# Keys' ends for two tiles at once, a norm product on VectorE, a bf16 bias and routing weights in eight transfers

## The chip, the cores and the metric

The kernel runs on one core of a Trainium2 chip. The metric is device time in microseconds (us), as the median of several executions. Besides the times there is one profiled execution, whose instructions, waits and transfers can be read one by one. The engines are called PE (TensorE), DVE (VectorE), ACT (ScalarE), POOL (GpSimd) and SP (SyncE, which here issues nearly all transfers).

## The reference

The input is 16 images of 64 x 64 pixels and 128 channels, in float32. Two layers follow each other; only the second is touched by the change.

```
x = x + deform(groupnorm(x))          # 3x3 convolution gives offsets, x is sampled there
t = tokens(x)                         # 4096 tokens of 128 channels per image
t = t + attn(layernorm(t))
t = t + experts(layernorm(t))

attn:    q, k, v = split(n @ w_qkv + b_qkv)      # 8 heads of 16 channels, per token
         a[i, j] = softmax_j(scale * q[i] * k[j])   # 16 x 16 scores within one head of one token
         out = (a @ v) @ w_proj + b_proj
experts: p = softmax over the tokens of n @ gate_w.T + gate_b      # 64 experts
         each expert pools its 8 best tokens by p, runs a two-layer network on the sum,
         and its output is added to those tokens, weighted by p
```

## The kernel before

**Stages.** `Images` goes through the 16 images: the first and the last as code of their own, the 14 between as the body of a loop (line 1261). `finish` then runs the experts' networks and adds their outputs. Setup (weights, masks, constants) stands in `Images.__init__`.

**Chunks and slots.** An image has 4096 pixels in `NCH` = 8 chunks of 512. A chunk takes 32 steps of the sampling, done two at a time: PE spreads the row coordinates (`yps` from `parts` and `sel`, bf16), ACT makes ramps of them (`rhat`) and of the column coordinates (`chat`, loaded by SP from `cc_d`), PE multiplies (`yps` from `rhat` and `xr`), DVE multiplies both (`prod`), and PE sums (`acc`). The convolution of the next chunk (`cbank`), the attention of the chunks before (`tokens`), the norm of the next image (`prep`) and the routing of the image before (`tail`) run beside it.

**Tokens of a chunk.** The 512 tokens are four tiles of 128 (`a` = 0 to 3). `tokens` transposes, adds the residual, normalizes, and for each tile multiplies by `wqkv` on PE (`qkv_mm`, into `bank` for even tiles and `bank2` for odd ones) and adds the bias on DVE (`qkv_add`). The softmax needs the largest score for each query. So `end(a, 0)` takes the smallest key of each head on DVE (`kmm`), `shift` subtracts it from the keys on POOL, `end(a, 1)` takes the largest shifted key, `tops` multiplies it by the query on POOL, and ACT's Relu makes the largest score of it (`top`). Then, for each half of a tile, POOL makes the 16 x 16 scores of four heads (two instructions of 128 x 1024 on `sc`), ACT takes the exponential, DVE sums (`den`), POOL weighs with the values (`ev`), and DVE sums again (`att`). Before `proj` the result is transposed; `proj` sums bias and product for each tile in PSUM, 32 output rows at a time (`by_columns`). A second layer norm (`layer_norm` with `dst`) needs -mean/std for each token (`nmr`): `root` computes the inverse deviation on POOL by a power (`rstd`) and then `nmr` in two more POOL instructions, and ACT applies both (`xln`).

**Routing.** `tail` finds each expert's 8 best tokens in `logits`, marks them in `big` (also called `mark` there), and scales eight blocks of 512 columns on ACT (`scale`). When all are scaled, one transfer stores all 64 x 4096 weights to `wt_d`.

**Order.** Nothing of an image is emitted as it is written. Every operation is recorded with a slot (32 to a chunk, one for each step of the sampling), and `Work.order` plans the image: each engine takes, of what is ready by the planner's own durations, what starts first, with the slot as a handicap (`HASTE`). Operations put in by `plan.together` stay together. The queues of the engines then run strictly in the planned order, SP's too. A change of a slot, or of an operation's size, therefore moves instructions on every engine. In the profile all of them carry line 203, where they are emitted, so groups must be told apart by their tiles. PE runs each float32 matmul as two instructions with a weight load each; the counts of the profile are of those.

Of the kernel before, what the change touches and what calls it, by code (L numbers as in the profile page):

```python
# [10 lines left out]
BF16 = mybir.dt.bfloat16  # L11
I32 = mybir.dt.int32
AF = mybir.ActivationFunctionType
ALU = mybir.AluOpType
AX = mybir.AxisListType
# [4 lines left out]
P = 128  # L20
B, IMG, C = 16, 64, 128
NPIX = IMG * IMG
# [4 lines left out]
HEADS, HD = 8, 16  # L27
# [19 lines left out]
def bcast(ap, axis, n):  # L47

    shape = list(ap.shape)
    return ap.unsqueeze(axis).to_broadcast(shape[:axis] + [n] + shape[axis:])  # L50


def at_image(ap, b):

    return ap[b : b + 1] if isinstance(b, int) else ap[ds(b, 1)]


def by_columns(nc, out, weights, moving, start=True, stop=True):

    for c in range(0, out.shape[0], 32):  # L60
        nc.tensor.matmul(
            out[c : c + 32], weights[:, c : c + 32], moving, start=start, stop=stop)
# [315 lines left out]
class Images:  # L378
# [8 lines left out]
    def __init__(self, ctx, tc, x, conv_w, conv_b, w_qkv, b_qkv, w_proj, b_proj, gate_w, gate_b,  # L387
# [3 lines left out]
        nc = tc.nc  # L391
# [8 lines left out]
        ps = ctx.enter_context(tc.tile_pool(name="imgp", bufs=1, space=PSUM))  # L400
# [7 lines left out]
        def keep(shape, name, dtype=F32):  # L408
            return cp.tile(shape, dtype, name=name)
# [12 lines left out]
        for v in range(4):  # L422
            for m in range(4):
                at, c = slice(32 * v + m, 32 * (v + 1), 4), channel(0, v, m)
# [18 lines left out]
        nc.vector.tensor_scalar(self.bqkv[:, 0], self.bqkv[:, 0], C ** -0.5, None, ALU.mult)  # L443
        self.wproj = keep([P, C], "wproj")
        nc.sync.dma_start(self.wproj, w_proj)
        self.bproj = keep([P, C], "bproj")
        nc.sync.dma_start(self.bproj, b_proj.partition_broadcast(P))
        graw = keep([E, C], "graw")
        nc.sync.dma_start(graw, gate_w)
        self.gb = keep([E, 1], "gb")  # L450
# [50 lines left out]
        for g in range(4):  # L501
            for t in range(3):
                at = 32 * g + 8 * t
# [17 lines left out]
                         stop=True)  # L521
# [5 lines left out]
        for o in range(2):  # L527
# [5 lines left out]
            for g in range(4):  # L533
                for r in range(2):
                    at = 32 * g + 24 + r
# [31 lines left out]
        for m in range(4):  # L567
            nc.vector.memset(self.red[m], 0.0)
            for v in range(4):
                a, h = divmod((v - m) % 4, 2)  # L570
                at = 14 + 16 * a + h
# [366 lines left out]
    def layer_norm(self, src, dst, plan, slot):  # L938


        nc, mv, rstd = plan, self.mv, self.rstd[dst is not None]

        def stats(a):
            nc.vector.bn_stats(self.lst[:, a, :], src[:, a, :])
            nc.vector.bn_aggr(mv[:, a, :], self.lst[:, a, :])

        def root():
            nc.gpsimd.tensor_scalar(rstd, mv[:, :, 1], LN_EPS, None, ALU.add)
            nc.gpsimd.tensor_tensor(rstd, rstd, self.half, ALU.pow)
            if dst is not None:  # L950
                nc.gpsimd.tensor_scalar(self.nmr, mv[:, :, 0], -1.0, None, ALU.mult)
                nc.gpsimd.tensor_tensor(self.nmr, self.nmr, rstd, ALU.mult)

        def scale(a):
            nc.scalar.activation(
                dst[:, a, :], src[:, a, :], AF.Identity, bias=self.nmr[:, a : a + 1],
                scale=rstd[:, a : a + 1])

        for a in range(NA):
            plan.add(slot + a // 2, lambda a=a: stats(a))  # L960
            if dst is not None:
                plan.add(slot + 2, lambda a=a: scale(a))
        plan.add(slot + 1, root)
# [4 lines left out]
    def tokens(self, b, k, slot, dense=False, alone=HEADS):  # L968
# [14 lines left out]
        def add(rel, fn):  # L983
            plan.add(slot + rel, fn)
# [30 lines left out]
        def heads(s, a):  # L1015
            return self.qkv[:, a, s].rearrange("p (h d) -> p h d", d=HD)

        def tile_of(ap, a):
            return ap[:, HEADS * a : HEADS * (a + 1)]

        def qkv_mm(a):
            by_columns(nc, (self.bank, self.bank2)[a % 2][:, : 3 * C], t1T[:, a, :], self.wqkv)

        def qkv_add(a):
            nc.vector.scalar_tensor_tensor(
                self.qkv[:, a].rearrange("p s c -> p (s c)"),
                (self.bank, self.bank2)[a % 2][:, : 3 * C], self.rstd[0][:, a : a + 1],
                self.bqkv.rearrange("p s c -> p (s c)"), ALU.mult, ALU.add)

        def end(a, i):
            nc.vector.tensor_reduce(
                tile_of(self.kmm[:, i, :], a), heads(1, a), AX.X, ALU.max if i else ALU.min)

        def shift(a):
            nc.gpsimd.tensor_tensor(
                heads(1, a), heads(1, a), bcast(tile_of(self.kmm[:, 0, :], a), 2, HD),
                ALU.subtract)

        def tops(a):
            nc.gpsimd.tensor_tensor(
                tile_of(top, a), heads(0, a), bcast(tile_of(self.kmm[:, 1, :], a), 2, HD),
                ALU.mult)


        def group(i):
# [28 lines left out]

        for a in range(NA):
            at = 8 * a
            plan.together(slot + at + 7.5, lambda: qkv_mm(a))
            add(at + 8, lambda: qkv_add(a))  # L1080
            add(at + 9, lambda: end(a, 0))
            add(at + 9.5, lambda: shift(a))
            add(at + 10, lambda: end(a, 1))
            add(at + 10.5, lambda: tops(a))
            add(at + 11, lambda: nc.scalar.activation(tile_of(top, a), tile_of(top, a), AF.Relu))
            for i in (2 * a, 2 * a + 1):
                add(12 + 4 * i, lambda: score(i))
                add(14 + 4 * i, lambda: expo(i))
                add(16 + 4 * i, lambda: weigh(i))
            add(at + 20, lambda: nc.vector.reciprocal(tile_of(den, a), tile_of(den, a)))  # L1090
            add(at + 23, lambda: divide(a))
# [6 lines left out]
        def proj():  # L1098
            for a in range(NA):
                ps = self.bank[:, P * a : P * (a + 1)]  # L1100
                by_columns(nc, ps, self.ident, self.bproj, stop=False)
                by_columns(nc, ps, attT[:, a, :], self.wproj, start=False)

        def second():
# [29 lines left out]
    def tail(self, b, slot, turns):  # L1134
# [25 lines left out]
        def scale(k):  # L1160
            ks = slice(CHW * k, CHW * (k + 1))
            nc.scalar.activation(mark[:, ks], mark[:, ks], AF.Identity, scale=self.rsum)

        plan.add(slot, best)
        plan.add(slot + 4, lambda: nc.vector.match_replace(mark, self.top8, logits, HUGE))
        for k in range(NCH):
# [1 line left out]
            plan.add(slot + 8 + 2 * k, lambda k=k: choose(k))  # L1168
            plan.add(slot + 25 + k, lambda k=k: scale(k))
        plan.add(slot + 24, total)  # L1170
        plan.add(slot + 33, lambda: nc.sync.dma_start(
            at_image(self.wt_d, b).rearrange("b e n -> (b e) n"), mark))


        def load(i):
# [16 lines left out]
        def add(i):  # L1192
            for g in range(2 * NA):
                by_columns(
                    nc, self.bank2[:, :E], self.xl[:, g // NA, g % NA, :],
                    self.wt[:, E * g : E * (g + 1)],
                    start=(g == 0), stop=(g == 2 * NA - 1))

        def keep(i):
            if i == 0:  # L1200
                nc.vector.tensor_copy(self.pool_sum, self.bank2[:, :E])
            else:
                nc.vector.tensor_tensor(self.pool_sum, self.bank2[:, :E], self.pool_sum, ALU.add)
            if i == NCH // 2 - 1:
                nc.vector.tensor_copy(
                    self.pooled[:, :, b : b + 1] if isinstance(b, int)
                    else self.pooled[:, :, ds(b, 1)], self.pool_sum.unsqueeze(2))
# [269 lines left out]
```

## Time and profile before

| | us |
|---|---|
| median of 3 runs | 9108.26 |
| lowest, highest | 9106.29, 9114.67 |
| the profiled execution | 9137.11 |
| its span, first to last instruction | 9135.3 |
| mean granted TensorE clock in it | 0.951 of full speed |

In a group's row, `out<-in` names the tiles, the sizes are partitions x elements, and behind the count stand the busy time in us, the mean ns of one instruction, and the idle time of the engine just before them with what ended most of it. In the timeline the first two columns are start and duration in us; equal instructions that follow each other are merged, and brackets hold the idle time before them and what ended it. In a table of stages the columns are the stage, its length, busy us of PE, PE's weight loads, DVE, ACT and POOL with the number of instructions, the granted clock, the DMA engines' busy share and GB/s. SPq is SP's queue, where transfers are issued.

The images fill the span from about 80 to 8690 us; the experts' stage takes the rest.

### The profile page before, as it was taken

To read this page: it belongs to the slowest core of one execution; us is meant where nothing else is said; L and a number is where in the kernel's file an instruction comes from. 1 tells how busy PE (TensorE), PEld (TensorE's weight loads), DVE (VectorE), ACT (ScalarE), POOL (GpSimd) and SP (SyncE) were. 2 spreads that over 40 slices of the span, in tenths; PEclk is the share of its full clock that TensorE was granted. 3 is DMA by queue.
4 is the path that set the end of the run, shared out by engine and by line. 5 is a ranking of instruction groups with operands and counts; after the bars stand their busy time and mean duration, and the time that the engine had idled before them with its cause. 6 is when DMAs were issued, how large, how long until landed. Compare 5 with 4: busy or idle time off the path is not lost. (4 is left out here: it accounts for less than half of the span.)

```text
span 9135.3 us, 466677 instructions
## 1 busy us (share of the span) xinstructions
PE 8158.9 (89%) x205574; PEld 4234.3 (46%) x205574; DVE 7263.5 (80%) x10177; ACT 6534.8 (72%) x8082; POOL 7620.6 (83%) x5699
## 2 busy tenths in 40 slices
PE   6999999999999999999999999999899999989464
PEld 3544445454454545444454544445454544544234
DVE  3888888888888888888888888888888888888713
ACT  3877777777777778777777777777777777778400
POOL 1988888989898998989889898989989898989700
PEclk8999999999999999999999999999999999999756
DMA  5766766766676666766666766667676666666278
GB/s 140 190 176 181 189 174 187 186 183 184 177 192 176 187 185 186 186 177 186 181 186 183 191 182 180 187 176 192 178 197 179 182 188 176 190 174 182 80 234 294
DMA packets 1048563, 1678.95 MB, mean 184 GB/s; under 512 B 442480, under 2 KB 660336, under 8 KB 1041328
## 3 DMA queue, kind: packets, MB, share of 16 engines
q1 hardware_dynamic: 1024688, 1613.25, 64.7%
q8 instruction: 1616, 26.48, 1.3%
q10 hardware_dynamic: 21760, 35.14, 1.1%
q14 instruction: 499, 4.09, 0.2%
HBM read 1378.68 MB, written 268.96 MB: 180 GB/s over the span
## 5 line engine op out<-in xcount | busy, mean ns | idle before, releaser
L203 DVE SCALAR_TENSOR_TENSOR prod<-chat,yps 128x1024 f32<-128x1024 f32 x2048 | 2462.8, 1205 | 746.0 <-PE yps L203 214.2
L203 ACT ACTIVATE rhat<-yps 128x1024 f32<-128x1024 f32 x2048 | 2088.3, 1021 | 1296.4 <-PE yps L203 1197.7
L203 PEld LDWEIGHTS yps<-rhat,xr 32*32 32x32 f32 x131072 | 2172.1, 104 | 1525.7 <-ACT rhat L203 703.2
L203 PE MATMUL yps<-rhat,xr 32*32 32x176 f32 (+1 forms) x131072 | 2590.3, 275 | 277.6 <-ACT rhat L203 187.1
L203 PE MATMUL cbank<-pad,wconv 128*32 128x512 f32 x18432 | 2526.2, 621 | 34.6 <-DVE far L203 27.2
L203 POOL TENSOR_TENSOR ev<-sc,qkv 128x1024 f32<-128x1024 f32 x1019 | 2424.8, 2380 | 125.7 <-ACT sc L203 115.4
L203 POOL TENSOR_TENSOR sc<-qkv 128x1024 f32<-128x1024 f32 x1019 | 1977.7, 1941 | 57.6 <-POOLq L1261 19.1
L203 POOL TENSOR_TENSOR sc<-sc,top 128x1024 f32<-128x1024 f32 x1019 | 1988.2, 1953 | 17.8 <-ACT top L203 5.9
L203 DVE TENSOR_REDUCE att<-ev 128x64 f32<-128x1024 f32 x1024 | 1235.5, 1206 | 119.5 <-POOL ev L203 71.9
L203 ACT ACTIVATE chat<-chat,cbi,csc 128x1024 f32<-128x1024 f32 x1024 | 1261.4, 1237 | 56.0 <-DMA chat<-cc_d 50.9
L203 DVE TENSOR_REDUCE den<-sc 128x64 f32<-128x1024 f32 x1024 | 1237.9, 1209 | 63.9 <-ACT sc L203 61.2
L203 ACT ACTIVATE sc<-sc 128x1024 f32<-128x1024 f32 x1024 | 1076.0, 1051 | 220.6 <-POOL sc L203 144.2
L203 PE MATMUL acc<-prod,red 128*32 128x512 f32 x8192 | 1156.0, 617 | 39.6 <-DVE prod L203 37.7
L203 ACT ACTIVATE chat<-chat,cbi 128x1024 f32<-128x1024 f32 x1024 | 1161.2, 1143 | 33.2 <-DMA chat<-cc_d 31.8
L203 PE MATMUL yps<-parts,sel 32*32 32x512 bf16 x16384 | 932.6, 390 | 194.6 <-DVE prod L203 167.9
L203 PEld LDWEIGHTS cbank<-pad,wconv 128*32 128x32 f32 x18432 | 487.3, 110 | 839.0 <-issue 729.4
L203 PEld LDWEIGHTS <-sel 32*32 32x32 bf16 x16384 | 293.4, 88 | 991.1 <-issue 952.4
L203 DVE RECIPROCAL den<-den 128x128 f32<-128x128 f32 x512 | 480.4, 938 | 6.5
L203 DVE SCALAR_TENSOR_TENSOR qkv<-bank,rstd,bqkv 128x384 f32<-128x384 f32 x512 | 312.3, 610 | 194.4 <-PE bank L203 181.1
L203 PE MATMUL bank<-wqkv,tr 128*32 128x384 f32 x4096 | 440.6, 497 | 14.5 <-DVE qkv L203 11.6
L203 POOL TENSOR_TENSOR qkv<-qkv,kmm 128x128 f32<-128x128 f32 x512 | 219.7, 429 | 217.4 <-DVE kmm L203 214.8
L203 PEld LDWEIGHTS acc<-prod,red 128*32 128x32 f32 x8192 | 185.9, 109 | 347.9 <-issue 286.4
(166 smaller groups left out, 7699.8 us busy)
## 6 DMA issues: line engine op xcount, KB each, us to landing
chat<-cc_d SPq DMA_DIRECT2D x8192, 128.0 KB
xr<-xn_d SPq DMA_DIRECT2D x512, 128.0 KB
pc_d<-pc SPq DMA_DIRECT2D x512, 96.0 KB
parts<-pc_d SPq DMA_DIRECT2D x512, 96.0 KB
xl<-in_x_dram SPq DMA_DIRECT2D x128, 256.0 KB
xres<-in_x_dram SPq DMA_DIRECT2D x256, 128.0 KB
xn_d<-wt SPq DMA_DIRECT2D x128, 256.0 KB
cc_d<-cd SPq DMA_DIRECT2D x128, 256.0 KB
```

Source lines behind the costliest of these rows:

```text
L203: getattr(engine, fn)(*args, **kwargs)
```

## The change

There are four edits.

- **Bias.** The bias of the projection was a float32 tile, broadcast to 128 partitions, and was multiplied by the identity. Now setup splits it into three bf16 values whose sum is the float32 one to rounding, in rows 0 to 2 of a bf16 tile that is otherwise zero, and PE multiplies that by a 128 x 32 tile of bf16 ones.
- **Norm product.** `nmr` is one DVE instruction in place of two of POOL.
- **Two tiles at once.** `end`, `shift`, `tops` and the Relu each handle tiles 0 and 1, or 2 and 3, in one instruction. The slots of `qkv_mm` and `qkv_add` of an odd tile move to one behind those of the even tile, and the second pair's slots move 3.7 earlier.
- **Eight transfers.** Each of the eight blocks of the routing weights is stored on its own, recorded right behind its scaling, and the one store is gone.

```diff
@@ -443,8 +443,18 @@
         nc.vector.tensor_scalar(self.bqkv[:, 0], self.bqkv[:, 0], C ** -0.5, None, ALU.mult)
         self.wproj = keep([P, C], "wproj")
         nc.sync.dma_start(self.wproj, w_proj)
-        self.bproj = keep([P, C], "bproj")
-        nc.sync.dma_start(self.bproj, b_proj.partition_broadcast(P))
+        self.bproj = keep([P, C], "bproj", BF16)
+        self.ones3 = keep([P, 32], "ones3", BF16)
+        nc.vector.memset(self.bproj, 0.0)
+        nc.vector.memset(self.ones3, 1.0)
+        rest = self.big[0:1, 3 * NPIX // 4 + P :][:, :C]
+        part = self.big.bitcast(BF16)[0:1, 2 * (3 * NPIX // 4 + P + C) :][:, :C]
+        nc.sync.dma_start(rest, b_proj.unsqueeze(0))
+        for i in range(3):
+            nc.vector.tensor_copy(part, rest)
+            nc.sync.dma_start(self.bproj[i : i + 1], part)
+            if i < 2:
+                nc.vector.tensor_tensor(rest, rest, part, ALU.subtract)
         graw = keep([E, C], "graw")
         nc.sync.dma_start(graw, gate_w)
         self.gb = keep([E, 1], "gb")
@@ -948,8 +958,8 @@
             nc.gpsimd.tensor_scalar(rstd, mv[:, :, 1], LN_EPS, None, ALU.add)
             nc.gpsimd.tensor_tensor(rstd, rstd, self.half, ALU.pow)
             if dst is not None:
-                nc.gpsimd.tensor_scalar(self.nmr, mv[:, :, 0], -1.0, None, ALU.mult)
-                nc.gpsimd.tensor_tensor(self.nmr, self.nmr, rstd, ALU.mult)
+                nc.vector.scalar_tensor_tensor(
+                    self.nmr, mv[:, :, 0], -1.0, rstd, ALU.mult, ALU.mult)
 
         def scale(a):
             nc.scalar.activation(
@@ -1015,8 +1025,8 @@
         def heads(s, a):
             return self.qkv[:, a, s].rearrange("p (h d) -> p h d", d=HD)
 
-        def tile_of(ap, a):
-            return ap[:, HEADS * a : HEADS * (a + 1)]
+        def tile_of(ap, a, n=1):
+            return ap[:, HEADS * a : HEADS * (a + n)]
 
         def qkv_mm(a):
             by_columns(nc, (self.bank, self.bank2)[a % 2][:, : 3 * C], t1T[:, a, :], self.wqkv)
@@ -1029,19 +1039,27 @@
 
 
 
+        def ends(a, i):
+            return tile_of(self.kmm[:, i, :], a, 2).rearrange("p (a h) -> p a h", a=2)
+
+        def both(s, a):
+            return self.qkv[:, a : a + 2, s].rearrange("p a (h d) -> p a h d", d=HD)
+
         def end(a, i):
-            nc.vector.tensor_reduce(
-                tile_of(self.kmm[:, i, :], a), heads(1, a), AX.X, ALU.max if i else ALU.min)
+            nc.vector.tensor_reduce(ends(a, i), both(1, a), AX.X, ALU.max if i else ALU.min)
 
         def shift(a):
             nc.gpsimd.tensor_tensor(
-                heads(1, a), heads(1, a), bcast(tile_of(self.kmm[:, 0, :], a), 2, HD),
-                ALU.subtract)
+                both(1, a), both(1, a), bcast(ends(a, 0), 3, HD), ALU.subtract)
 
         def tops(a):
             nc.gpsimd.tensor_tensor(
-                tile_of(top, a), heads(0, a), bcast(tile_of(self.kmm[:, 1, :], a), 2, HD),
-                ALU.mult)
+                tile_of(top, a, 2).rearrange("p (a h) d -> p a h d", a=2), both(0, a),
+                bcast(ends(a, 1), 3, HD), ALU.mult)
+
+        def signs(a):
+            v = tile_of(top, a, 2)
+            nc.scalar.activation(v, v, AF.Relu)
 
 
         def group(i):
@@ -1076,13 +1094,15 @@
 
         for a in range(NA):
             at = 8 * a
-            plan.together(slot + at + 7.5, lambda: qkv_mm(a))
-            add(at + 8, lambda: qkv_add(a))
-            add(at + 9, lambda: end(a, 0))
-            add(at + 9.5, lambda: shift(a))
-            add(at + 10, lambda: end(a, 1))
-            add(at + 10.5, lambda: tops(a))
-            add(at + 11, lambda: nc.scalar.activation(tile_of(top, a), tile_of(top, a), AF.Relu))
+            early = at - 7 * (a % 2) - 3.7 * (a > 1)
+            plan.together(slot + early + 7.5, lambda: qkv_mm(a))
+            add(early + 8, lambda: qkv_add(a))
+            if a % 2 == 0:
+                add(early + 9.1, lambda: end(a, 0))
+                add(early + 9.5, lambda: shift(a))
+                add(early + 10, lambda: end(a, 1))
+                add(early + 10.5, lambda: tops(a))
+                add(early + 11, lambda: signs(a))
             for i in (2 * a, 2 * a + 1):
                 add(12 + 4 * i, lambda: score(i))
                 add(14 + 4 * i, lambda: expo(i))
@@ -1098,7 +1118,9 @@
         def proj():
             for a in range(NA):
                 ps = self.bank[:, P * a : P * (a + 1)]
-                by_columns(nc, ps, self.ident, self.bproj, stop=False)
+                for c in range(0, P, 32):
+                    nc.tensor.matmul(
+                        ps[c : c + 32], self.ones3, self.bproj, start=True, stop=False)
                 by_columns(nc, ps, attT[:, a, :], self.wproj, start=False)
 
         def second():
@@ -1160,6 +1182,8 @@
         def scale(k):
             ks = slice(CHW * k, CHW * (k + 1))
             nc.scalar.activation(mark[:, ks], mark[:, ks], AF.Identity, scale=self.rsum)
+            nc.sync.dma_start(
+                at_image(self.wt_d, b).rearrange("b e n -> (b e) n")[:, ks], mark[:, ks])
 
         plan.add(slot, best)
         plan.add(slot + 4, lambda: nc.vector.match_replace(mark, self.top8, logits, HUGE))
@@ -1168,8 +1192,6 @@
             plan.add(slot + 8 + 2 * k, lambda k=k: choose(k))
             plan.add(slot + 25 + k, lambda k=k: scale(k))
         plan.add(slot + 24, total)
-        plan.add(slot + 33, lambda: nc.sync.dma_start(
-            at_image(self.wt_d, b).rearrange("b e n -> (b e) n"), mark))
 
 
         def load(i):
```

## The prediction

> **What bounds the kernel now.** I read the page's busy times first, then one image by itself, then the waits, and last the two places where the change is heaviest. On the page TensorE leads, and GpSimd is close behind it:
>
> ```profile
> PE 8158.9 (89%) x205574; PEld 4234.3 (46%) x205574; DVE 7263.5 (80%) x10177; ACT 6534.8 (72%) x8082; POOL 7620.6 (83%) x5699
> ```
>
> These shares mix the images with the setup and the expert stage. The copies into the tile norm start one image after the other, 526.8 to 532.8 us apart. The table of stages over one of these periods gives:
>
> ```profile
> core 0: us, PE busy (x) PEld busy (x) DVE busy (x) ACT busy (x) POOL busy (x), PEclk, DMA share, GB/s
> 4341.10:4870.70 529.60, 492.84 (x12744) 252.72 (x12740) 444.34 (x619) 407.20 (x505) 477.13 (x356) 0.98 0.68 184
> ```
>
> Idle per image: PE 37 us, POOL 52, DVE 85, ACT 122. Both PE and POOL are nearly full, so work taken from one alone would soon meet the other. PE is tighter, and the waits agree: ACT's largest wait is for PE (rhat <- PE yps, 1197.7 us in all), while PE waits 168 us for DVE's prod. I take PE as the bound and POOL as the next.
>
> Next, a place that recurs. In the timeline, the store of the routing weights is one transfer of 1024 KB, and PE stops soon after it:
>
> ```profile
> 4011.79 0.58 SPq L203 DMA_DIRECT2D wt_d<-big  x1
> ...
> 4016.84 1.04 PE L203 MATMUL yps<-rhat,xr 32*32 32x176 f32 x41
> ...
> 4017.88 1.93 POOL L203 TENSOR_TENSOR sc<-sc,top 128x1024 f32<-128x1024 f32 x1
> ...
> 4021.27 0.48 PE L203 MATMUL yps<-rhat,xr 32*32 32x80 f32 x23 [3.38 <-issue]
> ...
> 4021.86 1.22 DVE L203 SCALAR_TENSOR_TENSOR prod<-chat,yps 128x1024 f32<-128x1024 f32 x1 [4.40 <-issue]
> ```
>
> "issue" says that no semaphore held PE: 41 of 64 matmuls of one step had run, the other 23 came 3.38 us later. The stages around it:
>
> ```profile
> 4010.00:4014.00 4.00, 4.00 (x117) 1.88 (x120) 3.16 (x4) 3.82 (x6) 4.00 (x3) 1.00 0.86 247
> 4014.00:4018.00 4.00, 3.89 (x133) 2.12 (x110) 2.42 (x3) 4.00 (x6) 4.00 (x4) 1.00 1.01 252
> 4018.00:4021.20 3.20, 0.00 (x0) 0.00 (x0) 0.00 (x0) 1.14 (x2) 3.20 (x3) 1.00 0.88 243
> ```
>
> The DMA engines are full (1.01) from 4014 to 4018, and between 4009 and 4018 the DMA view has no packet of the instruction queue, which over the span brings one every 5.7 us (1616 packets). In each of the 14 images of the loop PE stops about 9.5 us after this store, for 2.5 to 3.9 us (median 3.4). I read it as instructions that came late behind the store; the trace shows the order, not the cause.
>
> **The change, part by part.** *Bias as bf16 rows.* Now each 32-column quarter multiplies a float32 identity by the broadcast bias. The timeline of one projection:
>
> ```profile
> 4257.42 0.40 PE L203 MATMUL bank<-wproj,tr 128*32 128x128 f32 x8
> ...
> 4257.64 0.40 PE L203 MATMUL bank<-bproj,ident 128*32 128x128 f32 x8
> ...
> 4257.86 0.40 PE L203 MATMUL bank<-wproj,tr 128*32 128x128 f32 x8
> ```
>
> Starts are 0.22 us apart, so the four bias groups of a chunk take 0.87 us; there are 8 chunks in 16 images, 128 in all. The new group has four bf16 instructions instead of eight. Float32 matmuls of 512 and 128 columns last 617 and 273 ns, 0.90 ns a column over a fixed 156; bf16 ones of 512 columns last 390, so about 0.46 ns a column by the same fixed part. That makes 128 x 0.46 = 58 ns a group, and saves 4 x (215 - 58) = 0.63 us a chunk: 80 us. If bf16 brings nothing but half the instructions, 4 x 108 = 0.43 us: 55 us. A penalty for changing type between groups I leave out, because bf16 sel matmuls and float32 mains of the same 32*32 tiling already start within 20 ns of each other (4016.82 and 4016.84). All of it is on PE, which sets the pace: -80.
>
> *Eight transfers.* The stores become 128 KB each, one behind each of ACT's eight scalings, which the built order spreads over 46 SP transfers. No burst of 1 MB is left, so I take the stall as gone: 14 x 3.4 = -47; 0 if it only moves. SP gets 112 more issues of 0.58 us, 64 us in all. They are moved in among the column loads (chat<-cc_d), and each now waits for its ACT scaling with those loads behind it. What covers this is SP's own slack: it waits 1408 us for DVE's prod to free column buffers. I charge 0; were the cover gone, the eight waits of an image would cost ACT and DVE what they wait for these loads now once more, 83 and 95 us together at most, of which I keep 30 for the range.
>
> *Ends, shift and largest scores for two tiles; the norm product.* The rows:
>
> ```profile
> L203 DVE TENSOR_REDUCE kmm<-qkv 128x8 f32<-128x128 f32 x1024 | 284.7, 278 | 29.9 <-POOL qkv L203 15.7
> L203 POOL TENSOR_TENSOR qkv<-qkv,kmm 128x128 f32<-128x128 f32 x512 | 219.7, 429 | 217.4 <-DVE kmm L203 214.8
> L203 POOL TENSOR_TENSOR top<-qkv,kmm 128x128 f32<-128x128 f32 x512 | 209.9, 410 | 23.1 <-DVE kmm L203 21.3
> L203 POOL TENSOR_SCALAR nmr<-mv 128x4 f32<-128x4 f32 x128 | 31.1, 243 | 8.9
> L203 POOL TENSOR_TENSOR nmr<-nmr,rstd 128x4 f32<-128x4 f32 x128 | 25.9, 202 | 10.6
> ```
>
> GpSimd takes 1941 ns for 1024 elements (sc<-qkv) and 429 for 128, so 1.69 ns an element: 256 elements cost 645 (shift) and 626 (tops). Saved: 220 - 256 x 0.645 = 55, 210 - 256 x 0.626 = 50, and 57 of nmr; 162 us on POOL, 10.1 an image. DVE's ends: 679 ns for 512 elements (far) against 278 for 128 give 1.04 an element, 412 for 256; 512 of them are 211 us, 74 less. ACT's Relu: 512 x 303 become 256 x 410 (slope from 1051 ns at 1024), 50 less, beside other work.
>
> PE loses 5.0 us an image from the bias and 3.4 from the stall, 8.4 together; POOL loses 10.1. The smaller relief decides, so POOL's saving earns nothing of its own but keeps POOL from taking over. That is also its cover: were POOL unrelieved, its 52 us idle would have to absorb 8.4.
>
> The new waits: the shift waits for both tiles' ends, and behind it on POOL stand the scores of the other group. The matmuls and additions of the second tile of a pair come earlier in the built order, next to the first's; no instruction of theirs is added. I charge 0 here and price it as a rival.
>
> The norm product now stands on DVE between rstd's power on POOL and xln on ACT, and behind it in DVE's queue stands prod, for which PE waits. It reads two SBUF operands. How such small instructions last here:
>
> ```profile
> L203 DVE TENSOR_TENSOR gmv<-gmv x32: 158/622/1853, 95.4 to 7912.4; 128x1 f32<-128x1 f32 x32
> ...
> L203 DVE TENSOR_TENSOR farthest<-farthest,most x16: 758/1522/1535, 533.6 to 8469.5; 128x1 f32<-128x1 f32 x16
> ...
> L1274 DVE TENSOR_TENSOR worst<-worst,farthest x1: 146/146/146, 8471.3 to 8471.3; 128x1 f32<-128x1 f32 x1
> ```
>
> The columns are shortest/median/longest in ns. The last, with GpSimd idle, takes 146 ns; the first two, of the same shape, up to 1853 beside a busy GpSimd. I take the mean of the two medians, 1.07 us: 128 x 1.07 = 137 us, so DVE ends 63 us above today, 4 an image against 85 idle. What reaches PE lies between 0 and 137. PE had to wait for prod at 173 of 2048 steps, so most delays should be absorbed; I charge a quarter, +34.
>
> A rule of the Trainium skill speaks against this edit: "SBUF — State Buffer", section "Who interferes with whom", says that a VectorE instruction with two SBUF inputs contends with a GpSimd instruction that reads SBUF, and that whoever is first holds the shared ports for its whole instruction. These three rows agree with it. By the rule alone each product could wait out a full score (1.94 us): an estimate of 128 x 1.94 = 248 us of DVE time.
>
> *Setup.* The bias is split into three rows through a chain of copies and transfers. In the built order three more SP issues (0.55 us each) and the first eight sel stores (4.97 us) stand ahead of the first image load, now at 24.48 us; the second, at 30.66, moves little. Between 2 and 7 us, once: +5.
>
> Sum: -80 - 47 + 34 + 5 = -88. The profiled execution has a span of 9135.3 and took 9137.1 us, 28.9 above the median of the three runs, 9108.3. By it the sum gives 9049; I carry the difference over to the median: 9108 - 88 = 9020.
>
> **The rivals.** *POOL sets the pace.* Then its 10.1 us an image count, and the stall too, since after it POOL waits 4.7 us for mv: 13.5 x 15.5 = -209, 8899. For it: the 236 us that POOL waits for kmm should shrink with half the handshakes. Against: POOL idles more than PE.
>
> *The pair comes late.* The first score of a pair waits for the second tile too: 0.85 us of matmuls (wqkv), 0.61 of qkv addition, 0.13 of longer reduction, 1.6 us. POOL waited for kmm in 139 of 1024 cases; if a quarter of 256 pairs show the whole, +102, which eats the gain: 9122.
>
> *The product blocks DVE (slower).* Each product waits out a GpSimd instruction and PE waits for the prod behind it: 128 x 1.85 = 237 in place of the 34: 9108 - 122 + 237 = 9223. It decides from 122 / 128 = 0.95 us a chunk that reaches PE. For it: POOL is busy 90% of an image, and its next instruction starts as soon as the power is done. Against: DVE's 85 us of idle time.
>
> **How the numbers follow.** The forecast has 0.57, with its own range of 8960 to 9080 (bias 55 instead of 80, the stall half or wholly gone, the product 0 to 80). POOL sets the pace: 0.17. The late pair: 0.16, spread over 0.03 faster, 0.08 same, 0.05 slower. The blocked DVE: 0.10, slower. A measurement of this kernel tells about 0.2%, 18 us, from no change. Faster 0.57 + 0.17 + 0.03 = 0.77; same 0.08; slower 0.15. The range reaches from POOL's case, 8905, to just past the late pair, 9130.
>
> **What would show it.** Right: bias groups about 0.06 us apart from the wproj group behind them; no PE gap of 2 us or more marked issue behind a wt_d store; nmr on DVE near 1 us; POOL busy near 467 us an image; periods near 524. Wrong: periods unchanged with PE idle above 45 us, which would point at the pair (POOL qkv <- DVE kmm up) or at nmr (above 1.5 us, PE <- DVE prod up); or a stall of like size at another store or load.

## The result, and the profile after

The changed kernel takes 9148.87 us (median of 6 runs, 9134.15 to 9163.08), the kernel before 9109.19 (6 runs, 9106.29 to 9117.26). The ratio is 1.0043, 95% interval 1.003 to 1.0056: slower by 0.4%, where I forecast 1% faster.

The profiled execution of the changed kernel took 9146.53 us, 2 below its median; that of the kernel before, 9137.11, stands 28 above its own. So the two traces differ by 9 us only, and comparing them understates the loss. The kernel before took 9130 to 9141 us at the median on the five chips of the experiments below, so 9137 is an ordinary time for it there; on which chip its trace was taken the record doesn't say. The runs carry the verdict, and the traces are read for where time lies.

The page's busy times after:

```profile
PE 8113.1 (89%) x203526; PEld 4178.5 (46%) x203526; DVE 7306.4 (80%) x9800; ACT 6534.0 (71%) x7826; POOL 7481.9 (82%) x4931
```

PE has 46 us less to do and POOL 139 less, as the edits intended. Now the groups that the prediction priced (out<-in with sizes, count | busy, mean ns | idle before them):

```profile
L203 DVE TENSOR_REDUCE kmm<-qkv 128x16 f32<-128x256 f32 x512 | 212.4, 415 | 11.4 <-POOL qkv L203 3.1
...
L203 POOL TENSOR_TENSOR qkv<-qkv,kmm 128x256 f32<-128x256 f32 x256 | 165.4, 646 | 177.0 <-DVE kmm L203 176.8
L203 POOL TENSOR_TENSOR top<-qkv,kmm 128x256 f32<-128x256 f32 x256 | 160.1, 625 | 10.0 <-DVE kmm L203 9.8
...
L203 ACT ACTIVATE top<-top 128x256 f32<-128x256 f32 x256 | 106.2, 415 | 65.8 <-POOL top L203 65.3
```

415, 646, 625 and 415 ns, against 412, 645, 626 and 410 worked out beforehand. The projection in the timeline of PE:

```profile
4255.00 0.24 PE L203 MATMUL bank<-bproj,ones 128*32 128x128 bf16 x4
4255.07 0.39 PE L203 MATMUL bank<-wproj,tr 128*32 128x128 f32 x8
4255.28 0.23 PE L203 MATMUL bank<-bproj,ones 128*32 128x128 bf16 x4
4255.34 0.39 PE L203 MATMUL bank<-wproj,tr 128*32 128x128 f32 x8
4255.56 0.23 PE L203 MATMUL bank<-bproj,ones 128*32 128x128 bf16 x4
```

A bias group starts 0.06 or 0.07 us ahead of the product behind it, where it was 0.22. The instructions cost what was forecast, then. One period between two norm copies in the middle shows that this was not enough (columns as in the table of stages before):

```profile
4344.20:4876.67 532.47, 490.26 (x12664) 250.16 (x12664) 446.03 (x594) 407.24 (x488) 467.45 (x307) 0.97 0.65 182
```

To compare whole images, I take the time from the first prod of an image to the first prod of the next, mean over the 14 images of the loop: 529.5 us before, 532.7 after. In it PE is busy 491.9 before and 489.9 after, its idle time goes from 37.6 to 42.8; POOL's busy time falls from 477.2 to 468.7, its idle time grows from 52.3 to 64.1. The first and the last image, which are code of their own, gained 10.2 and 12.3 us, and what follows the last prod is 11.1 us shorter, for a reason that was not looked for. The loop body lost 3.2 us in each of its 14 rounds, 45 us. The waits before (us in all, times, longest):

```profile
PE yps L203 <- DVE prod L203: 167.9, 173, 3.9
...
POOL ev L203 <- ACT sc L203: 115.4, 190, 1.4
...
POOL cd L203 <- ACT pc L203: 93.1, 31, 28.9
...
PE yps L203 <- issue: 84.7, 85, 3.9
```

And after:

```profile
PE yps L203 <- DVE prod L203: 274.2, 229, 5.2
...
POOL ev L203 <- ACT sc L203: 190.3, 151, 4.3
...
POOL qkv L203 <- DVE kmm L203: 176.8, 95, 6.0
...
POOL cd L203 <- ACT pc L203: 163.0, 79, 28.2
...
PE yps L203 <- issue: 29.1, 47, 2.2
```

PE's wait marked issue fell from 84.7 to 29.1 us. The trace before has a stop of 2.5 to 3.9 us behind the store in each of 14 images; after, five such stops of 1.5 to 2.2 us are left, which end 3 to 4 us behind one of the small stores. POOL's wait for kmm fell, from 214.8, with half as many shifts. But PE waits more for prod, and POOL more for ACT's scores and for ACT's pc. The largest single piece of the new wait for prod is an instruction of the routing that the change doesn't touch; the timeline of after:

```profile
3931.79 4.41 DVE L203 MAX8 top<-logits 64x8 f32<-64x4096 f32 x1
...
3936.12 1.19 DVE L203 TENSOR_REDUCE den<-sc 128x64 f32<-128x1024 f32 x1
...
3937.35 0.95 DVE L203 RECIPROCAL den<-den 128x128 f32<-128x128 f32 x1
...
3938.22 1.16 DVE L203 SCALAR_TENSOR_TENSOR prod<-chat,yps 128x1024 f32<-128x1024 f32 x1
...
3939.43 0.63 PE L203 MATMUL yps<-parts,sel 32*32 32x512 bf16 x8 [5.16 <-DVE prod L203]
```

Ahead of one prod DVE does MAX8, a sum and a reciprocal, and PE stands for 5.16 us; with the shorter gaps within 4 us of MAX8, PE loses 6.4 us at this place in every image of the loop, against 4.7 before. That suggested the theory for the experiments: each edit is worth about what was priced, and the loss comes from the new planned order of the loop body. The first rival: the joint instructions themselves hold up the softmax. The second: the norm product blocks DVE.

### The profile page after: what moved, and what is told of

Its sections match the earlier page's. It is cut to its first block, busy times and chain, and to the rows that moved or that the text cites. A ratio compares the mean times of both kernels' runs of the same rounds, so it can differ in the third digit from the quotient of the medians.

```text
span 9144.7 us, 461934 instructions
## 1 busy us (share of the span) xinstructions
PE 8113.1 (89%) x203526; PEld 4178.5 (46%) x203526; DVE 7306.4 (80%) x9800; ACT 6534.0 (71%) x7826; POOL 7481.9 (82%) x4931
## 5 line engine op out<-in xcount | busy, mean ns | idle before, releaser
L203 PE MATMUL yps<-rhat,xr 32*32 32x176 f32 (+1 forms) x131072 | 2622.2, 279 | 221.4 <-ACT rhat L203 185.3
L203 PE MATMUL yps<-parts,sel 32*32 32x512 bf16 x16384 | 969.5, 393 | 319.4 <-DVE prod L203 274.2
L203 DVE SCALAR_TENSOR_TENSOR cd<-cbank,cb,iot 128x256 f32<-128x256 f32 x512 | 223.8, 475 | 177.1 <-PE cbank L203 177.0
L203 DVE SCALAR_TENSOR_TENSOR qkv<-bank,rstd,bqkv 128x384 f32<-128x384 f32 x512 | 302.0, 605 | 74.3 <-PE bank L203 69.3
```

Source lines behind the costliest of these rows:

```text
L203: getattr(engine, fn)(*args, **kwargs)
```

## The experiments

Kernels of one group of runs are compared with the kernel before on the same chip, whose median was between 9130 and 9141 us there. A ratio below 1 is faster. "Loop" is the mean time per image of the loop, 529.5 in the profile before.

### Each edit alone

Every one of these is the kernel before with one of the four edits as in the diff above, planned anew (the planner makes its order for it). The bias:

```diff
-                by_columns(nc, ps, self.ident, self.bproj, stop=False)
+                for c in range(0, P, 32):
+                    nc.tensor.matmul(
+                        ps[c : c + 32], self.ones3, self.bproj, start=True, stop=False)
```

> Before with the bias edit alone, the images planned anew. Theory 'order' (each edit shortens its own work, but the planner puts the instructions of the loop's images in a new order that stalls more): the time is anywhere from -80 to +60 us, and the period of the loop's images (529.5 us before) moves against the straight-line images 0 and 15. Theory 'own cost' (one of the edits costs time by itself, the others gain what was forecast): -80 us, the 14 periods near 524.5. PE busy falls by 2 us or more an image in both.

Measured: 9086.40 against 9134.21, ratio 0.995 (0.9937 to 0.9964), 48 us faster. PE's busy time per image fell by 4.9 us, which is the priced 80 us over 16 images, but the loop fell only by 3.0: PE's idle time rose from 37.6 to 39.4.

The norm product:

```diff
-                nc.gpsimd.tensor_scalar(self.nmr, mv[:, :, 0], -1.0, None, ALU.mult)
-                nc.gpsimd.tensor_tensor(self.nmr, self.nmr, rstd, ALU.mult)
+                nc.vector.scalar_tensor_tensor(self.nmr, mv[:, :, 0], -1.0, rstd, ALU.mult, ALU.mult)
```

> Before with the norm product alone moved to VectorE, planned anew. Order: between -40 and +60 us with no relation to the product's own duration, which stays near 0.5 us (it was 0.54 in the changed kernel). Own cost with the product as the culprit: +40 us or more, PE's wait for prod up by 3 us an image or more in the stretches where a product stands.

Measured: 9127.96, ratio 0.9997 (0.9987 to 1.0007), no difference. The product's median was 0.69 us, DVE's busy time rose by 6.7 us an image.

Two tiles at once:

```diff
-            add(at + 9, lambda: end(a, 0))
-            add(at + 9.5, lambda: shift(a))
...
+            early = at - 7 * (a % 2) - 3.7 * (a > 1)
...
+            if a % 2 == 0:
+                add(early + 9.1, lambda: end(a, 0))
+                add(early + 9.5, lambda: shift(a))
...
```

> Before with ends, shift, tops and Relu for two tiles at once alone, planned anew. Order: between -60 and +60 us. Own cost with the pair as the culprit: +40 us or more, POOL's wait for kmm above the 14.0 us an image of before. Forecast as it was (POOL -6.5 us an image, nothing lost): about 0 to -50.

Measured: 9201.58, ratio 1.007 (1.0056 to 1.0083), 67 us slower. POOL's waits in it:

```profile
POOL cd L203 <- ACT pc L203: 191.6, 56, 29.0
POOL ev L203 <- ACT sc L203: 165.2, 127, 3.8
POOL qkv L203 <- DVE kmm L203: 133.4, 73, 3.7
POOL ev L203 <- DVE att L203: 114.7, 57, 3.8
```

The wait of the shift for the ends, which the rival of the late pair should have raised, fell by 81 us against the kernel before. POOL waits in other places instead.

The eight stores:

```diff
+            nc.sync.dma_start(
+                at_image(self.wt_d, b).rearrange("b e n -> (b e) n")[:, ks], mark[:, ks])
...
-        plan.add(slot + 33, lambda: nc.sync.dma_start(
-            at_image(self.wt_d, b).rearrange("b e n -> (b e) n"), mark))
```

> Before with the eight stores alone, planned anew. The 3.4 us stop of PE behind the one store is gone in both theories. Own cost: -47 us, or, if the eight stores hold up the column loads behind them, about +40 with DVE's and ACT's waits for chat<-cc_d up by 3 us an image. Order: -47 is not reached, without those waits going up.

Measured: 9081.27, ratio 0.9949 (0.9936 to 0.9963), 53 us faster; PE's wait marked issue at yps fell from 84.7 to 38.3 us.

The four sum to -48 - 6 + 67 - 53 = -40 us. The whole change measured +40. So the pair is the one edit that loses, but the edits do not add up either.

### Is it the joint instructions, or their place in the order?

Only the slots of the additions and matmuls moved, all instructions as before:

```diff
-            plan.together(slot + at + 7.5, lambda: qkv_mm(a))
-            add(at + 8, lambda: qkv_add(a))
+            early = at - 7 * (a % 2) - 3.7 * (a > 1)
+            plan.together(slot + early + 7.5, lambda: qkv_mm(a))
+            add(early + 8, lambda: qkv_add(a))
```

> Before with the earlier slots of the wqkv products and the qkv additions alone (odd tiles next to even ones, second pair 3.7 earlier); ends, shift, tops and Relu stay single. Theory 'slots' (the move of the matmuls and additions, and the new order that follows, makes the loss of the pair edit alone, which was +64 us): +40 us or more. Theory 'merged' (the joint instructions do it: the first score waits for two tiles, and POOL, with less to do, only waits elsewhere): within 20 us of before.

Measured: 9147.22 against 9140.87, ratio 1.0006 (0.9997 to 1.0015): no loss to be seen from the slots alone, as the theory 'merged' had it.

The pair without moving the second pair forward:

```diff
-            early = at - 7 * (a % 2) - 3.7 * (a > 1)
+            early = at - 7 * (a % 2)
```

> The pair edit alone, with the odd tile's slots 7 earlier but without the 3.7 for the second pair. Slots: between 0 and +64 us, nearer to 0, since two tiles of four keep their place. Merged: +40 us or more, as with the 3.7.

Measured: 9165.37 against 9140.87, ratio 1.0032 (1.0021 to 1.0043), 24 us slower. With the 3.7 it was 1.007, 67 us: a shift of the slots that changes no instruction costs the larger part, as the theory 'slots' had it.

The order planned for the pair kept, but each joint instruction issued as the two of before, one behind the other:

```diff
+            op = nc.gpsimd.tensor_tensor(
+                both(1, a), both(1, a), bcast(ends(a, 0), 3, HD), ALU.subtract)
+            op.instead = "gpsimd", [("tensor_tensor", (
+                heads(1, c), heads(1, c), bcast(tile_of(self.kmm[:, 0, :], c), 2, HD),
+                ALU.subtract), {}) for c in (a, a + 1)]
...
```

> The pair edit alone, with its planned order kept, but wherever a joint instruction of two tiles stands two single ones are issued behind each other. Merged: the loss of +64 us goes away, mostly, since the first tile's scores no longer wait for the second tile's shift. Order: it stays at +64 or goes up, to +100, by the 6.5 us an image that POOL has more to do.

Measured: 9185.87 against 9139.65, ratio 1.0049 (1.0035 to 1.0062), 46 of the pair's 67 us; the intervals of the two overlap. Most of the loss stays when the joint instructions are gone and their order is left, so they are not the main cause as instructions. Its expectation says that the run frees the first tile from waiting for the second; it doesn't, as POOL still runs both shifts ahead of the pair's first scores. What speaks against the late pair is POOL's shorter wait for the ends, 118.9 us here and 133.4 in the pair.

### The order by itself

The planner's constant `HASTE`, the weight of the slots, changes the order and nothing else. In the kernel before, 40 became 38 and 42:

```diff
-HASTE = 40
+HASTE = 38
```

> Before with the planner's weight of a slot (HASTE) 38 instead of 40: the same instructions, in another order. Theory 'order': the order alone moves the time by 20 to 60 us either way, as much as the losses to be explained. Theory 'merged' (the joint instructions of the pair edit cost by themselves): within 20 us of before.

> The same with HASTE 42. Order: 20 to 60 us either way. Merged: within 20 us.

Measured: with 38, 9273.51 against 9139.65, ratio 1.0147 (1.0132 to 1.0163); with 42, 9141.44, ratio 1.0005 (0.9996 to 1.0014), no difference. With 38 the same instructions in another order lose 134 us, more than any edit gained or lost; not every new order does so. The waits with 38:

```profile
POOL ev L203 <- ACT sc L203: 273.6, 257, 6.6
...
PE yps L203 <- DVE prod L203: 145.9, 148, 2.0
...
PE yps L203 <- DVE ntop L203: 76.6, 15, 5.1
```

The last row is new: PE stands behind the routing on DVE 15 times, for up to 5.1 us. POOL's wait for ACT's scores has more than doubled.

Then the changed kernel with all four edits, and 42:

```diff
-HASTE = 40
+HASTE = 42
```

> The changed kernel with HASTE 42: the same four edits in another order. Order: the time moves by 20 to 100 us, either way, as before with HASTE 38 did (+134), and with it falls or rises PE's wait for prod (17.3 us an image). If the edits themselves cost: within 20 us of the changed kernel.

Measured: 9082.09 against 9130.37, ratio 0.9948 (0.9936 to 0.996), 48 us faster. These are the four edits unaltered, and the sign has turned. The changed kernel itself was not run again on this chip; with one instruction moved it took 9163.15 there (next run). In the traces the loop takes 527.9 us an image, 4.8 less than in the changed kernel. PE's busy time is the same (490.1 and 489.9), and so is the granted clock (0.97); its idle time fell from 42.8 to 37.8. The waits:

```profile
POOL qkv L203 <- DVE kmm L203: 231.1, 108, 6.6
...
POOL cd L203 <- ACT pc L203: 205.2, 90, 28.8
...
PE yps L203 <- DVE prod L203: 192.6, 148, 5.6
...
POOL ev L203 <- ACT sc L203: 75.7, 113, 2.6
```

PE's wait for prod is back at 192.6 from 274.2; POOL's wait for pc is longer than in the slower kernel, so that wait, by its length alone, is not what cost the time. What PE loses around the two long routing instructions (MAX8 and MATCH_REPLACE8) is 2.9 us an image here, 6.4 in the changed kernel.

The changed kernel with MAX8 alone taken out of the planned order and put behind the next prod:

```diff
+        for op in [op for op in result if op.calls[0][0] == "max"]:
+            at = result.index(op)
+            for n in range(at + 1, min(at + 60, len(result))):
+                if "prod" in result[n].calls[0][1][0].tensor.name:
+                    result.insert(n, result.pop(at))
+                    break
         return result
```

> The changed kernel with its planned order kept but for one instruction: DVE's search for the eight best of 4096 logits (MAX8, 4.41 us, once an image) is moved behind the next prod, for which PE waits 5.16 us at this place in each of the loop's 14 images. Theory 'stops at places' (the loss of the new order is the sum of such stops, and each removed one is won): the 5.16 us stop falls to 2 us or less, and the time by 30 to 60 us. Rival 'all is tied' (a stop removed here turns up at another place): the stop falls, the time stays within 15 us.

Measured: 9163.15 against 9130.37, ratio 1.0041 (1.0028 to 1.0055), as slow as the changed kernel. The one stop of 5.16 us became several shorter ones, of at most 3 us, 4.5 to 6.4 us together within 4 us of MAX8. So that stop, the plainest line of the trace, is not the cause by itself.

### The edits in the order of the kernel before

Here the planner sees the operations of before, and each is replaced when it is issued; a store is issued twelve recorded operations behind its scaling. The product:

```diff
+                first = nc.gpsimd.tensor_scalar(self.nmr, mv[:, :, 0], -1.0, None, ALU.mult)
+                second = nc.gpsimd.tensor_tensor(self.nmr, self.nmr, rstd, ALU.mult)
+                first.instead = "vector", []
+                second.instead = "vector", [("scalar_tensor_tensor", (
+                    self.nmr, mv[:, :, 0], -1.0, rstd, ALU.mult, ALU.mult), {})]
```

> The norm product alone on VectorE, with the planned order of before kept: at the place of POOL's second nmr instruction. If the three edits with the kept order lost 74 us through this product (it lasted 1.47 us at the median there, 0.47 in the changed kernel): +80 us or more. If they lost through the stores or the bias: within 30 us.

Measured: 9180.43 against 9139.65, ratio 1.005 (1.0036 to 1.0063), 41 us slower. The product's instructions (shortest/median/longest ns):

```profile
L205 DVE SCALAR_TENSOR_TENSOR nmr<-mv,rstd x128: 149/1455/2030, 288.4 to 8675.0; 128x4 f32<-128x4 f32 x128
...
  DVE nmr L205: 170.0, 94
```

In this order the product takes 1.46 us at the median and 1.07 in the mean (136.3 us in all), and ACT waits 170 us for it. What makes it long can be read in the timeline:

```profile
4002.75 1.93 POOL L205 TENSOR_TENSOR sc<-sc,top 128x1024 f32<-128x1024 f32 x1
...
4003.24 1.47 DVE L205 SCALAR_TENSOR_TENSOR nmr<-mv,rstd 128x4 f32<-128x4 f32 x1
```

The product starts while POOL makes scores and ends at 4004.71, 0.03 us after them. That is no chance: 93 of the 128 products here last over 0.6 us, and every one ends 17 to 24 ns after an instruction of POOL on scores or values (`sc`, `ev`). In the changed kernel 52 do, and all end 15 to 22 ns after an instruction of POOL. There the product's row is this:

```profile
L203 DVE SCALAR_TENSOR_TENSOR nmr<-mv,rstd x128: 98/474/2151, 282.4 to 8653.9; 128x4 f32<-128x4 f32 x128
```

The same instruction takes a third at the median, and half in the mean (0.54 us). The 41 us lie between the two outcomes expected. The second rival, that the product costs time, is real in one order; in the other the product is short.

Bias, product and stores together, planned anew and in the old order:

```diff
+                    nc.tensor.matmul(
+                        ps[c : c + 32], self.ones3, self.bproj, start=True, stop=False)
...
+                nc.vector.scalar_tensor_tensor(
+                    self.nmr, mv[:, :, 0], -1.0, rstd, ALU.mult, ALU.mult)
...
+            nc.sync.dma_start(
+                at_image(self.wt_d, b).rearrange("b e n -> (b e) n")[:, ks], mark[:, ks])
```

> The changed kernel without the pair edit: bias, norm product and eight stores, planned anew. If the pair edit alone makes the loss: the sum of the three alone, -46 -3 -50 = about -100 us (ratio 0.989). If any further edit on top upsets the loop's order (theory 'order'): -60 us or less of a gain, with new waits in the loop's images.

> The same three edits, but with the planned order of before kept: the planner is given the old operations and durations, and only when they are issued are the bias matmuls replaced by bf16 ones, the second of POOL's nmr instructions by the one on VectorE (the first left out), and the one store by eight, each 12 recorded operations behind its scaling. Order: faster than the version planned anew. Edits by themselves, with order of no account: the same, about -100 us. If the product on VectorE costs by itself, less of a gain than the two others alone, -96.

Measured: 9075.13 against 9140.87, ratio 0.9936 (0.9922 to 0.9949), and in the old order 9214.77, ratio 1.0086 (1.0072 to 1.0099). Planned anew, the gain of 66 us is short of the 107 that the three made alone. I had taken the old order for the safe one; it is 140 us worse.

Bias and stores, planned anew and in the old order:

```diff
+                    nc.tensor.matmul(
+                        ps[c : c + 32], self.ones3, self.bproj, start=True, stop=False)
...
+            nc.sync.dma_start(
+                at_image(self.wt_d, b).rearrange("b e n -> (b e) n")[:, ks], mark[:, ks])
```

> The bias and the eight stores alone, planned anew. If the two gains stand beside each other: -46 - 50 = -96 us against before. If the order takes a part, as with all three (-66): -50 to -70. It would be the fastest of the kernels in the first case.

> The bias and the eight stores with the planned order of before kept. The three edits in this order cost +74, the product alone +41 in it. If the two others gain in the old order what they gained planned anew: about -96. If the loss of the three comes from the stores in the old order, too: 0 to +40, with DVE's and ACT's waits for chat<-cc_d up.

Measured: planned anew, 9045.74 against 9130.37, ratio 0.9912 (0.9897 to 0.9926), 85 us faster and the fastest of all kernels here. In the old order 9190.07, ratio 1.0064 (1.0051 to 1.0077). The middle period of the fast one:

```profile
4290.68:4814.47 523.79, 483.19 (x12616) 246.68 (x12608) 445.01 (x619) 408.76 (x505) 477.83 (x356) 0.98 0.66 186
```

POOL is not relieved at all here, and is less idle than in the changed kernel (46 us against 65). The relief of POOL was not needed for this gain.

Which of the two loses in the old order? The bias alone (its matmuls as above) and the stores alone:

```diff
+            nc.scalar.activation(
+                mark[:, ks], mark[:, ks], AF.Identity, scale=self.rsum).behind = (
+                "sync", [("dma_start", (
+                    at_image(self.wt_d, b).rearrange("b e n -> (b e) n")[:, ks], mark[:, ks]), {})])
```

> The bias rows in bf16 alone, every instruction in the order of the kernel before. Theory (the fixed-order version of bias and stores lost 60 us because eight stores stand in SP's queue ahead of loads that ScalarE waits for): without the stores the bias keeps its gain, 30 to 50 us below the kernel before, and ScalarE's wait for the loads of chat stays near 83 us in the execution. Rival (any edit that is left in the old order loses, because every other instruction then comes out of step): 0 to 40 us above the kernel before.

> The eight stores of the routing weights alone, every instruction in the order of the kernel before, each store twelve recorded operations behind its scaling. Theory (their place in SP's queue holds the loads of parts and chat): 60 to 110 us above the kernel before, ScalarE's wait for the loads of chat near 160 us in the execution, TensorE's stop of 3.4 us behind the large store gone all the same. Rival (the stores are harmless wherever they stand, the loss came with the bias): 30 to 50 us below the kernel before.

Measured: the bias 9120.47 against 9136.74, ratio 0.998 (0.9971 to 0.9989), 16 us faster; the stores 9206.81, ratio 1.0067 (1.0054 to 1.0081), 70 us slower. The bias in the old order lowers PE's busy time by 4.1 us an image, and the loop not at all (529.5): its gain lies in the first and the last image (10.7 and 4.9 us in the traces). That was less than the theory wanted and more than its rival. The stores, from the lists of ACT's and PE's waits:

```profile
ACT chat L205 <- DMA chat<-cc_d: 221.2, 103, 12.8
```

```profile
PE yps L205 <- DMA parts<-pc_d: 54.5, 43, 3.8
PE yps L205 <- issue: 41.3, 77, 1.5
```

PE's stop behind the large store is gone here too (41.3 with a longest of 1.5). But ACT waits 221 us for the loads of chat, from 82.7, once 12.8 us at a stretch, and PE waits 54.5 us for parts, for which it did not wait measurably before. These loads stand behind the stores in SP's queue. SP's own waits in this run:

```profile
SPq L205 <- DMA wt_d<-big: 102.1, 70, 3.9
...
SPq L205 <- ACT big L205: 3.0, 9, 0.5
```

So a store hardly ever waits for its scaling. It waits until the store before it, to the same tensor, has landed, 102.1 us in all, and holds up the loads behind it meanwhile. In the run of the stores planned anew this wait is 5.3 us, longest 0.6, and those stores gained 53 us.

In the old order the parts nearly add up: bias and stores make -16 + 70 = +54 us, and +60 was measured; with the product +95, and +74 was measured.

## Why the prediction was wrong

**Durations: right but for the product.** The joint instructions came out within 5 ns of the values worked out, the bias groups at 0.06 us, the product at 0.54 us in the mean where I took 1.07; POOL's busy time is 468.7 us an image in place of 467.

**Bias, -80: mis-sized.** The work left PE as priced, but only 48 us reached the time when planned anew and 16 in the old order. "All of it is on PE, which sets the pace" is a step that failed. PE was idle 37.6 us an image before, largely in waits for ACT and DVE, and part of what its matmuls saved turned into more of such waits: its idle time rose by 1.8 us an image planned anew, and by 4.1 in the old order, which is all that was saved there.

**Eight stores, -47: right** (53 alone), and the stop is tied to the large transfer, since it goes with it in both orders. It begins about 6 us behind the store and ends 9.5 us behind it, where I wrote that PE stops 9.5 us after. That instructions came late is not shown: in the trace before, two other stretches of 9 us or more without an instruction packet stand in nearly every image of the loop, and PE has no such stop there. "I charge 0" for SP's queue was right only for the planned place. At another place it cost about 120 us (from -53 to +70), and not by the wait for the scalings that I named: SP waited for the landing of one store after the other.

**Norm product, +34:** 6 us faster alone, within the interval of no difference, and 41 us slower in the old order. The 137 us of DVE time that I took were met in the old order (136.3), by luck, since a mean of two medians stood for a group that is partly short and partly long; in the order of the changed kernel it was 69.3 us. One row was misread: the addition of 146 ns ran with GpSimd busy, not idle, just as one of POOL's instructions gave way to the next. The Trainium skill's rule ("SBUF — State Buffer", section "Who interferes with whom") fits: all long products end right behind an instruction of POOL. The page states that one engine holds the ports for a whole instruction where VectorE runs in its two-port modes; here an instruction with two SBUF inputs shows it. The estimate worked out from the rule, 248 us, was not reached: 79 of the 128 products in the old order took under 1.5 us.

**Setup, +5:** nothing of it shows; the first norm copy comes 1.6 us earlier.

**POOL, "the smaller relief decides":** failed. With POOL relieved by 8.5 us an image and PE's own work shortened, the time should have fallen by the smaller of the two. POOL's idle time rose by 11.8 us an image and PE's by 5.2 instead. The rival that POOL sets the pace ends with it. Relief of busy time sets no lower limit to a gain when neither engine is full and each waits for the others.

**The order: the failed step that decided, and that I charged nothing.** I wrote that the pair's matmuls and additions come earlier and that "no instruction of theirs is added. I charge 0 here", and looked at how they moved only for the late-pair rival. Every edit made the planner rearrange the loop body, and that body runs 14 times: 3.2 us an image in the traces stand against 10 to 12 us gained in each of the images with an order of their own. That order alone can do it is shown by the kernel before with another `HASTE` (+134 us), and that it did turn this change's sign by the same four edits with 42 (-48). Between the changed kernel and its version with 42 the order is worth 5.0 us of PE's idle time an image. Against the rivals: the late pair would raise POOL's wait for kmm, which fell; the blocked DVE would need products of 1.85 us, and they took 0.54.

**The ranges.** The forecast's own range, 8960 to 9080, doesn't follow from the terms in its brackets: with the 5 of the setup they give 8986 to 9114. And POOL's case is 8899 in one place and 8905 in the other. The measured 9149 lies above all of these.

**What stays open.** No single wait of the new order was found that carries the loss: removing the longest stop changed nothing. Part of it shows in the busy time of PE, too: in the pair alone PE is busy 495.9 us an image with the same matmuls that took 491.9, with the granted clock at 0.97 in place of 0.98 over the loop; whether the clock or less overlap of matmuls does this, these runs do not separate. The changed kernel was measured on the chip of the result alone, so its +40 us stand beside edits that were measured on other chips, where the kernel before takes 21 to 32 us more. If the trace before was taken on such a chip, that would account for the 28 us by which it stands above its median; this is not shown.

## What to carry to other kernels

Where a planner orders the queues, the price of an edit is its own instructions plus a new order of everything else. Here the second ranged over more than 100 us, while most durations of the first were known to within a few ns. So measure an edit over a few settings of the planner before judging it, and do not take the old order as the safe one. Busy time that is taken from an engine which waits part of the time need not count in full: of 4.9 us an image taken from PE here, 3.0 reached the loop in one order, and of 4.1 nothing in another.

## What the hardware showed that I had not expected

- One DVE instruction on 128 x 4 elements took from 98 to 2381 ns; its median was 474 in one order, 694 in another and 1455 in a third. Whenever it took over 600 ns, it ended 15 to 25 ns after an instruction of POOL did.
- Matmuls in bf16 and float32 alternating on the same 128*32 tiling cost nothing extra: groups of four bf16 instructions took 0.05 to 0.07 us, and the float32 groups between them 0.21 to 0.22, as before.
- A 1 MB store by one transfer went with a stop of PE of about 3.4 us, which ended 9.5 us after its issue, in all 14 images; as eight transfers of 128 KB it left five stops of at most 2.2 us in the changed kernel and none above 1.5 us in the stores' run in the old order.
- In that run SP waited, up to 3.9 us at a time, for the landing of one small store before it issued the next, and ACT once waited 12.8 us for a load behind them.
